# Two adaptive-layernorm layers: moving the clamps, the scaled weights and some statistics to other places of a hand-written order

## The chip, the cores and the metric

One Trainium2 chip; the program runs on one of its cores. The core has TensorE (matrix products; PE in the profile, PEld for its weight loads), VectorE (DVE), ScalarE (ACT), GpSimd (POOL) and SyncE (SP, which here only issues DMAs). The metric is the device time of one execution in microseconds (us); of several runs the median counts.

## The reference

The input x has 8 batches of 512 tokens with 256 features, in float32. Two layers follow each other, each with an attention part and a feed-forward part:

- mod = silu(c) @ wmod gives for each batch six vectors of 256: sa, ca, ga, sb, cb, gb. ga and gb are clamped away from zero: (2 (g >= 0) - 1) * max(|g|, 0.25).
- attention part: h = layernorm(x) * (1 + ca) + sa; x = x + ga * attn(h)
- feed-forward part: h = layernorm(x) * (1 + cb) + sb; x = x + gb * ffn(h)

Layer 0's attention is h + [linear attention, window attention] @ Wout, after an RMS norm of h with the weight norm_w; the linear part has 16 heads of 16 with quadratic features and a causal sum, the window part a softmax over 64 earlier tokens. Since its first term is h itself, layer 0 computes x + ga * h and ga * (...) @ Wout as separate pieces. Its feed-forward part mixes each token with the one before it and computes sigmoid(xr Wr) * (relu(xk Wk)^2 Wv). Layer 1's attention is a causal softmax with rotary positions and a projection. Its feed-forward part is four products through 1024 hidden features.

## The kernel before, in words

The kernel holds one batch at a time in SBUF, 128 tokens or 128 features to a partition. Layer 0 runs through 16 units (a batch and one half of its heads), ten steps each; layer 1 through 32 units of six steps. Three PSUM tiles of two banks (`sc`) take scores and two of one bank (`mm`) take everything else.

The order of all this work is written out by hand. `when(time, what)` (L327) puts a closure on a list, with a time in steps of layer 0; `when1` (L330) does so with steps of layer 1, which begin at layer 0's step 160. At the end the list is sorted by time and carried out under `tc.manual_schedule()` (L1509), so each engine gets its instructions in that order, and each SyncE or GpSimd DMA too. An engine carries out its own instructions strictly in that order; between engines, semaphores make each instruction wait for the data that it needs and for the buffer that it overwrites. The numbers are places in an order and not times.

Batch b of layer 0 begins at step t0 = 20 b. Around it stand:

- `fetch` (L386, x from memory at t0 - 24.5, with the rows sa, ca, ga in `bc` from b = 2 on), `normed` (L349: statistics L357, a reciprocal root by ACT in L339 and L340, its refinement by five small VectorE instructions L344 to L347 and L363, the normalisation L371 on ACT or L373 on VectorE), `modulated` (L420: GpSimd multiplies and adds rows in L429, then forms ga * h in L431 and adds it to x in L433; in batch 0 the first two are VectorE's, L425 and L427), `squares` (L441), the RMS scale `hr` (L453 on VectorE in batch 0, L457 on GpSimd later), the transposes of hr (L468), the projections (L102, copied by `whole` to `qf` in L490) and the value copies `vs` (L543).
- `step` (L667): linear scores (L561), which ACT squares (L572) and GpSimd masks (L576), and window scores (L594), whose row maxima VectorE takes (L605); window weights (L638, ACT L648, GpSimd L658). `lin_values` (L701) and `win_values` (L724) are the products with the values.
- `finish` (L764): `scaled_weights(0)` at t0 + 26.0 fetches ga of the batch, spread over all partitions, into the tile `br` (SyncE, L772) and lets GpSimd form ga * Wout (L775) for the products L798 at t0 + 34.6 to 35.85, which L808 adds to x; `scaled_weights(1)` at t0 + 41.2 does the same with gb and the feed-forward weight. Both use the one `br` tile. `out_of` adds the feed-forward result to x by GpSimd (L908) and writes x to memory (`x_mid`, SyncE, L912, at t0 + 49.4).

The vectors mod are formed in a prologue at steps -22 to 2. The pieces ga and gb of all batches lie as 8x512 rows in `stash`; `clamped_batches(layer)` (L262) clamps them with four VectorE instructions (L220 to L223) and writes them to `mod_dram`, from where `fetch_ga` and `scaled_weights` read. Batch 0's ga is clamped apart, from PSUM, at -12.05. In front of all of that GpSimd sets the ones in four tiles (`vones`, `vswap`: L313, L319) and multiplies the weights Wq, Wk and Wv by norm_w (L317).

Layer 1's `prepare1` (L1047) fetches x by a GpSimd DMA (L1053), and uses `normed` with places of its own (`early` for batches 0 and 1, `usual` for the others); scores are L1214 and L1272, with maxima L1225, the shifted queries `qs` (L1256), ACT's exponentials L1283 and GpSimd's masks L1287; rotations are L1134 and L1139, value products L1306. The first steps of layer 1 run between the last ones of layer 0. After step 192 of layer 1 comes a feed-forward stage that is a long row of TensorE products (L1568).

Of the kernel before, what the change touches and what calls it, by code (L numbers as in the profile page):

```python
# [13 lines left out]
ALU = mybir.AluOpType  # L14
# [4 lines left out]
B, T, D = 8, 512, 256  # L19
H, HD = 16, 16  # L20
NTB = T // P
NC = D // P
# [8 lines left out]
def bcast(ap, shape, axis):  # L31
    return ap.unsqueeze(axis).to_broadcast(list(shape))
# [3 lines left out]
def adaln_two_layers_kernel(ctx: ExitStack, tc: tile.TileContext, t, out):  # L36
    nc = tc.nc
# [3 lines left out]
    def load(pool, name, shape, src, eng=None):  # L41
        dst = pool.tile(list(shape), FP, name=name, tag=name)
        (eng or nc.sync).dma_start(out=dst, in_=src)
        return dst
# [92 lines left out]
    with ExitStack() as lctx:  # L137
# [36 lines left out]
        wq, wk, wv = (wqkv0[:, :, i * D : (i + 1) * D] for i in range(3))  # L174
        normw = load(rp, "normw", [P, NC], t["norm_w_cols"])
# [38 lines left out]
        mod_b = rp.tile([P, NC, T], FP, name="mod", tag="df")[:B, 0, :]  # L214
        clamps = rp.tile([P, NC, T], FP, name="clamps", tag="xk")

        def clamp(dst, src):
            p, n = src.shape
            neg, sgn = clamps[:p, 0, :n], clamps[:p, 1, :n]
            nc.vector.tensor_scalar(neg, src, -1.0, 0.25, ALU.mult, ALU.max)  # L220
            nc.vector.tensor_tensor(neg, neg, src, ALU.max)
            nc.vector.tensor_scalar(sgn, src, 0.0, 2.0, ALU.is_ge, ALU.mult)
            nc.vector.scalar_tensor_tensor(dst, sgn, -1.0, neg, ALU.add, ALU.mult)  # L223

        def mod_product(ps, weights, layer, col, n):

            w, o = wm[layer][col // T], col % T
            for k in range(NC):
                nc.tensor.matmul(ps, weights[:, k, :], w[:, k, o : o + n], start=(k == 0), stop=(k == NC - 1))
# [9 lines left out]
        def by_batches(layer):  # L239
            if layer == 0:  # L240
                ps = got0["rows"] = sc.tile([P, 2, T], FP, name="sc", tag="sc")
                mod_product(ps[:B, 0, :], sT[0], 0, 0, T)
                ps = ps[:B, 1, :]
            else:
                ps = got0["rows"] = mm.tile([P, T], FP, name="mm", tag="mm")
                ps = ps[:B]
            for i, v in enumerate((2, 5)):
                mod_product(ps[:, i * D : (i + 1) * D], sT[layer], layer, v * D, D)

        stash = rp.tile([P, NC, T + 1], FP, name="stash", tag="hf")  # L250
# [8 lines left out]
        def copied_batches(layer):  # L259
            nc.scalar.copy(stash[:B, layer, :T], got0["rows"][:B, 1, :] if layer == 0 else got0["rows"][:B])  # L260

        def clamped_batches(layer):  # L262
            dst = mod_b if layer else mod_a[:, 2:4, :].rearrange("p v d -> p (v d)")
            clamp(dst, stash[:B, layer, :T])
            nc.sync.dma_start(
                out=mod_dram[:, 2 + 2 * layer : 4 + 2 * layer, :], in_=dst.rearrange("p (v d) -> p v d", d=D)
            )
# [42 lines left out]

        vones = [wp.tile([P, NTB, H, 32], FP, name=f"vo{i}", tag=f"vo{i}") for i in range(2)]
        vswap = [rp.tile([P, NTB, H // 2, 32], FP, name=f"vs{i}", tag=f"vs{i}") for i in range(2)]
        nc.gpsimd.memset(vones[0], 1.0)  # L313

        for w in (wq, wk, wv):
            for k in range(NC):
                nc.gpsimd.tensor_scalar(w[:, k, :], w[:, k, :], normw[:, k : k + 1], None, ALU.mult)  # L317
        for v in (vswap[0], vones[1], vswap[1]):
            nc.gpsimd.memset(v, 1.0)  # L319

# [4 lines left out]
        def when(time, what):  # L327
            plan.append((min(time, END0) + STEP0 * max(time - END0, 0.0), len(plan), what))
# [20 lines left out]
        def normed(when, x, first, at_root, last, name, by_act=True):  # L349

            held = {}

            def stats(j):
                if j == 0:
                    held["st"] = tok.tile([P, NTB, 6], FP, name="st", tag="st", bufs=2)
                    held["mv"] = tok.tile([P, NTB, 2], FP, name="mv", tag="mv", bufs=2)
                nc.vector.bn_stats(held["st"][:, j, :], x()[:, j, :])  # L357
                nc.vector.bn_aggr(held["mv"][:, j, :], held["st"][:, j, :])

            def spread():  # L360
                better(held, held["mv"][:, :, 1], 1e-5)
                off = held["off"] = tok.tile([P, NTB], FP, name="off", tag="off", bufs=2)
                nc.vector.scalar_tensor_tensor(off, held["mv"][:, :, 0], -1.0, held["r"], ALU.mult, ALU.mult)  # L363

            def norm(j):
                if j == 0:
                    held["x"] = tok.tile([P, NTB, D], FP, name=name, tag=name)
                dst, src = held["x"][:, j, :], x()[:, j, :]
                r, off = held["r"][:, j : j + 1], held["off"][:, j : j + 1]
                if by_act:  # L370
                    nc.scalar.activation(dst, src, AF.Identity, bias=off, scale=r)  # L371
                else:
                    nc.vector.tensor_scalar(dst, src, r, off, ALU.mult, ALU.add)  # L373

            for j in range(NTB):
                when(first[j], lambda j=j: stats(j))
                when(last[j], lambda j=j: norm(j))
            when(at_root, lambda: root(held, held["mv"][:, :, 1], eps5))
            when(at_root + 0.25, spread)
            return held  # L380

        def prepare(b):
            t0 = 20 * b
# [20 lines left out]
            when(t0 - 24.5, fetch)  # L404
            if b == 1:
                when(t0 - 31.9, fetch_rows)
                when(t0 - 15.9, fetch_ga)
            ln = normed(
                when,
                lambda: xs0[b],  # L410
# [353 lines left out]
        def finish(b):  # L764

            t0 = 20 * b
# [3 lines left out]
            def scaled_weights(i):  # L770
                bc = rp.tile([P, 1, D], FP, name="br", tag="br")
                nc.sync.dma_start(out=bc, in_=mod_dram[b, 2 + i : 3 + i, :].partition_broadcast(P))  # L772
                w, n = ((wout, 4), (wfv, 2))[i]
                held["w", i] = rp.tile([P, n, D], FP, name=f"ws{i}", tag=("xr", "ws1")[i])
                nc.gpsimd.tensor_tensor(held["w", i], w, bcast(bc[:, 0, :], [P, n, D], 1), ALU.mult)  # L775

            when(t0 + 26.0, lambda: scaled_weights(0))
            when(t0 + 41.2, lambda: scaled_weights(1))

            def features(c):  # L780
# [143 lines left out]
        for m in range(2 * B):  # L924
            t0 = 10 * m
# [12 lines left out]
            when(t0 + 20.45, lambda m=m: win_values(m))  # L938

        when(-22.0, on_every_row)  # L940
        when(-21.9, lambda: by_batches(0))
        for i, at in enumerate((-21.85, -13.65, -12.1)):
            when(at, lambda i=i: folded(i))
        for i, at in enumerate((-21.8, -21.7, -12.5, -12.4, -10.3, -6.4)):
            when(at, lambda i=i: mod_features(i))
        when(-12.05, lambda: clamp(ga_all, got0["f"][:, 1, :D]))
        when(-12.0, kept_batches)
        when(-10.4, lambda: copied_batches(0))
        when(1.6, lambda: by_batches(1))
        when(2.05, lambda: copied_batches(1))  # L950
        when(4.05, lambda: clamped_batches(0))
        when(4.95, lambda: clamped_batches(1))
        for b in range(B):
            prepare(b)
            finish(b)
# [91 lines left out]
        def prepare1(b):  # L1047

            t0 = 24 * b
# [3 lines left out]
                nc.gpsimd.dma_start(out=xs1[b], in_=x_mid[b].rearrange("(j p) d -> p j d", p=P))  # L1053


            early = ((135.5, (138.7, 0.3), 139.75, (142.15, 0.4)), (153.0, (164.2, 0.3), 165.6, (166.2, 0.2)))
            usual = (t0 - 37.0, (t0 - 33.6, 1.0), t0 - 29.4, (t0 - 28.6, 0.6))
            if b == 2:
                usual = (*usual[:3], (t0 - 28.9, 0.25))
            if b == 3:  # L1060
                usual = (t0 - 35.6, (t0 - 32.4, 0.6), *usual[2:])
            begin, (first, more), at_root, (last, apart_) = (early + (usual,))[min(b, 2)]
# [131 lines left out]
            for j, at in ((0, t0 + 6.45), (2, t0 + 9.45)):  # L1194
                if b == 0:
                    at = (6.7, 8.7)[j // 2]
# [219 lines left out]
        for b in range(B):  # L1416
            prepare1(b)
            project_out(b)
            for m in range(3 * b, min(3 * b + 3, len(raws))):
                at = 50 + 6 * m  # L1420
                when1(at, lambda m=m: look(m))
                for i in range(2):
                    when1(at + 5.6 + i, lambda m=m, i=i: low_bits(m, i))
# [10 lines left out]
        t0 = 24 * B  # L1434
# [286 lines left out]
```

## Time and profile before

| what | value |
| --- | --- |
| median of three runs | 1816.61 us (1813.01 to 1821.35) |
| profiled execution, its own time | 1810.34 us |
| its span, first to last instruction | 1808.6 us |
| mean granted TensorE clock | 0.993 |
| TensorE busy | 1742.7 us, 96% |
| VectorE, ScalarE, GpSimd busy | 1079.5, 887.3, 722.1 us |
| prologue and first steps, 0 to 90 us | TensorE busy 72.2 us |
| the rest of layer 0, 90 to 630 us | TensorE busy 523.6 us |
| both layers' steps together, 630 to 720 us | TensorE busy 79.5 us |
| layer 1's attention, 720 to 1200 us | TensorE busy 466.4 us |
| feed-forward stage, 1200 to 1808 us | TensorE busy 601.1 us |

A row of a timeline gives the start and the length in us, the engine, the line, the operation, the tiles written and read, the shapes and how many instructions are merged; in brackets stands the idle time in front of the row and who ended it. A row of the table by windows gives the window, its length, the busy time of TensorE, its weight loads, VectorE, ScalarE and GpSimd (instructions in brackets), then the granted TensorE clock as a share of the full one, the share of the DMA engines and GB/s.

### The profile page before, as it was taken

The numbers are of one execution on the slowest core, as the hardware profiler recorded it, in microseconds if no ns is written. First come the engines' busy times: TensorE is split into PE (matmuls) and PEld (weight loads), VectorE is DVE, ScalarE is ACT, GpSimd is POOL, SyncE is SP. The second block draws the span as 40 slices with busy tenths as digits, with TensorE's granted clock in tenths as the row PEclk, the third lists the DMA queues.
The fourth block names the chain that finished last, engine by engine and source line by source line (L and its number), as shares of the span: only waits on it lengthen the run. The fifth ranks groups of instructions, "written<-read, shape, count | busy, mean of one in ns | idle before, by whom it ended". The sixth has DMA issues, their size and how long they took to land.

```text
span 1808.6 us, 41155 instructions
## 1 busy us (share of the span) xinstructions
PE 1742.7 (96%) x16886; PEld 1191.8 (66%) x16886; DVE 1079.5 (60%) x3708; ACT 887.3 (49%) x1276; POOL 722.1 (40%) x1098
## 2 busy tenths in 40 slices
PE   7899999999999988999999999999999999999998
PEld 4456666665666654544555455688888888888887
DVE  5556574756656566578888887435354553635352
ACT  3666666766667645566666665413122222313221
POOL 4675866768576663456655555500000000000000
PEclk9999999999999999999999999999999999999999
DMA  4100101011001101023121110520000000000000
GB/s 149 41 14 6 37 5 37 5 38 33 12 17 35 40 5 39 1 66 117 51 74 52 61 48 30 190 59 27 1 27 26 1 27 1 27 1 27 0 13 14
DMA packets 43029, 65.59 MB, mean 36 GB/s; under 512 B 4152, under 2 KB 33592, under 8 KB 42832
## 3 DMA queue, kind: packets, MB, share of 16 engines
q1 hardware_dynamic: 37648, 46.62, 8.0%
q0 software_dynamic: 5184, 16.25, 3.0%
q8 instruction: 134, 2.20, 0.5%
q14 instruction: 63, 0.52, 0.1%
HBM read 50.24 MB, written 12.63 MB: 35 GB/s over the span
## 4 chain that ended last, share of the span: by engine, by line
PE 56%; ACT 3%; POOL 3%; DVE 2%; issue 1%; DMA 0%; ACTq 0%; POOLq 0%; DVEq 0%
PE mm L1568 31%; PE sc L1272 7%; PE mm L1306 4%; PE mm L1631 3%; PE mm L1124 2%; PE mm L1364 2%; PE mm L1182 2%; PE sc L1214 1%; ACT at L1283 1%; POOL flat L1139 1%; PE sc L1474 1%; POOL at L1287 1%; PE mm L1248 1%; PE mm L798 1%; ACT k L1146 1%
## 5 line engine op out<-in xcount | busy, mean ns | idle before, releaser
L1568 PE MATMUL mm<-gh,h 128*128 128x512 f32 x1024 | 398.1, 390 | 1.8 <-issue 1.8
L1568 PE MATMUL mm<-gl,h 128*128 128x512 f32 x1024 | 397.5, 389 | 0.0
L1225 DVE CUSTOM_DVE_ANT_0 junk<-sc,cmask 128x256 bf16<-128x256 f32 (+3 forms) x512 | 225.2, 487 | 93.5 <-PE sc L1214 90.0
L131 DVE CAST gh<-row 128x512 fp32r<-128x512 f32 x192 | 82.1, 431 | 257.9 <-ACT row L1614 132.3
L1283 ACT ACTIVATE at<-sc 128x768 f32<-128x768 f32 (+1 forms) x192 | 168.8, 882 | 113.9 <-PE sc L1214 101.3
L1568 PEld LDWEIGHTS mm<-gh,h 128*128 128x128 f32 x1024 | 192.2, 188 | 41.9 <-issue 2.2
L1568 PEld LDWEIGHTS mm<-gl,h 128*128 128x128 f32 x1024 | 192.2, 188 | 39.7
L658 POOL TENSOR_SCALAR_AFFINE_SELECT aw<-aw 64x512 f32<-64x512 f32 (+1 forms) x320 | 168.5, 553 | 97.5 <-ACT aw L648 93.8
L572 ACT ACTIVATE at<-sc 128x768 f32<-128x768 f32 (+1 forms) x192 | 164.0, 883 | 65.8 <-PE sc L561 65.1
L1214 PE MATMUL sc<-k,q 32*128 32x512 f32 (+3 forms) x1024 | 190.6, 469 | 5.8 <-ACT at L1283 4.5
L1272 PE MATMUL sc<-qs,k 32*128 32x384 f32 (+3 forms) x1024 | 188.6, 468 | 1.7 <-DVE qs L1256 1.7
L1287 POOL TENSOR_SCALAR_AFFINE_SELECT at<-at 128x256 f32<-128x256 f32 x256 | 103.5, 417 | 186.4 <-ACT at L1283 186.0
L605 DVE CUSTOM_DVE_ANT_0 junk<-sc,wmask 128x128 bf16<-128x128 f32 x512 | 115.3, 285 | 82.6 <-PE sc L594 82.5
L576 POOL TENSOR_SCALAR_AFFINE_SELECT at<-at 128x256 f32<-128x256 f32 x256 | 104.7, 430 | 110.6 <-ACT at L572 109.8
L1620 ACT ACTIVATE row<-mm,h_s_cols 128x512 f32<-128x512 f32 x64 | 44.1, 689 | 194.3 <-PE mm L1568 194.3
L132 DVE TENSOR_TENSOR gl<-row,gh 128x512 fp32r<-128x512 f32 x185 | 127.0, 689 | 7.3
L1272 PEld LDWEIGHTS sc<-qs,k 32*128 32x128 f32 x1024 | 81.3, 184 | 68.4 <-DVE maxima L1225 35.2
L1614 ACT ACTIVATE row<-mm,h_s_cols 128x512 f32<-128x512 f32 x64 | 44.2, 690 | 155.8 <-PE mm L1568 155.7
L561 PE MATMUL sc<-qm,qk 32*128 32x512 f32 (+3 forms) x1024 | 100.3, 470 | 2.4 <-ACT qq L503 1.0
L1214 PEld LDWEIGHTS sc<-k,q 32*128 32x128 f32 x1024 | 82.1, 184 | 14.1 <-ACT at L1283 9.7
L1608 ACT ACTIVATE sg<-mm,w_s_cols 128x512 f32<-128x512 f32 x56 | 38.6, 689 | 103.6 <-PE mm L1568 95.8
L648 ACT ACTIVATE aw<-sc 128x1024 f32<-128x1024 f32 (+1 forms) x64 | 62.2, 972 | 43.7 <-PE sc L638 42.3
(249 smaller groups left out, 3532.8 us busy)
## 6 DMA issues: line engine op xcount, KB each, us to landing
x_mid<-x SPq DMA_DIRECT2D x16, 512.0 KB, 3.0
x<-x_mid POOLq DMA_DIRECT2D x9, 512.0 KB, 4.3
raw<-in_h1T_dram SPq DMA_DIRECT2D x8, 512.0 KB, 3.4
raw<-in_h2T_dram SPq DMA_DIRECT2D x8, 512.0 KB, 3.4
h<-in_h1T_dram POOLq DMA_DIRECT2D x8, 512.0 KB, 7.2
h<-in_h2T_dram POOLq DMA_DIRECT2D x8, 512.0 KB, 7.7
out_dram<-tmp SPq DMA_DIRECT2D x16, 256.0 KB, 2.8
x<-in_L_attn_x_dram SPq DMA_DIRECT2D x7, 512.0 KB, 4.5
```

The source lines that it names most:

```text
L132: (rest or nc.vector).tensor_tensor(parts[1], src, parts[0].bitcast(FP), ALU.subtract)
L561: lambda i=i, r=r, kb=kb, n=n, o=o: nc.tensor.matmul(ps[:, i, o : o + n], k[r, e, kb * P : (kb + 1) * P], qm[r, e, kb * P : T], start=True ...
L572: nc.scalar.activation(at, ps[:, :, :o], AF.Square, scale=0.5)
L576: nc.gpsimd.affine_select(out=d, in_=d, pattern=[[0, 2], [1, P]], compare_op=ALU.is_ge, fill=0.0, base=0, channel_multiplier=-1,)
L605: nc.vector.tensor_tensor_reduce(junk, ps[:, i, ii * P : (ii + 1) * P], wmask[:, int(blk > 0), :], -1.0, BIG, ALU.add, ALU.min, maxima[:, ...
L658: nc.gpsimd.affine_select(out=d, in_=d, pattern=[[0, d.shape[1]], [sign, 64]], compare_op=ALU.is_ge, fill=0.0, base=0, channel_multiplier= ...
L1214: nc.tensor.matmul(ps[:, i, o : o + m], q[r, e, qb * P : (qb + 1) * P], k[r, e, :m], start=True, stop=True,)
L1225: nc.vector.tensor_tensor_reduce(junk[:, :m], ps[:, i, o : o + m], got1["cmask"][:, T - m :], -1.0, BIG, ALU.add, ALU.min, maxima[:, NTB * ...
L1272: nc.tensor.matmul(ps[:, i, o : o + m], k[r, e, kb * P : (kb + 1) * P], qs[r, kb * P : T], start=True, stop=True)
L1283: nc.scalar.activation(at, ps[:, :, :o], AF.Exp, scale=0.25)
L1287: nc.gpsimd.affine_select(out=d, in_=d, pattern=[[0, 2], [1, P]], compare_op=ALU.is_ge, fill=0.0, base=0, channel_multiplier=-1,)
L1568: nc.tensor.matmul(ps, w[:, k, col : col + P], part[:, k, :], start=(k == 0 and i == 0), stop=(k == n - 1 and i == len(parts) - 1),)
```

## The change

It moves work to other places of the order; what is computed stays the same, and no instruction is added or taken away.

- The four memsets of ones stand together; the scalings of Wq and Wk come into the list at -20.2 and that of Wv at -11.1, behind the sums of batch 0.
- Layer 0's clamp goes from 4.05 to -2.7, layer 1's from 4.95 to four places between 5.45 and 7.1, one instruction each, behind the copy qf (5.35).
- Batch 1's ga is read at -2.6 instead of 4.1.
- ga * Wout, with its DMA, goes from t0 + 26.0 to t0 + 30.3 for all batches but the last. That is behind hr, L431 and L433 of batch b + 2 (t0 + 27.4 to 28.8), behind the second L908 and the x_mid write of batch b - 1 (t0 + 29.4); for batch 6 also behind two loads of layer 1 (146.2, 150.0).
- In layer 1 the statistics, roots and, for batch 2, the fetch and the normalisations get other places.

```diff
-        def clamp(dst, src):
+        def clamp(dst, src, steps=range(4)):
...
+            for i in steps:
...
-        def clamped_batches(layer):
+        def clamped_batches(layer, *steps):
             dst = mod_b if layer else mod_a[:, 2:4, :].rearrange("p v d -> p (v d)")
-            clamp(dst, stash[:B, layer, :T])
+            clamp(dst, stash[:B, layer, :T], steps)
+            if 3 not in steps:
+                return
...
-        nc.gpsimd.memset(vones[0], 1.0)
-
-        for w in (wq, wk, wv):
-            for k in range(NC):
-                nc.gpsimd.tensor_scalar(w[:, k, :], w[:, k, :], normw[:, k : k + 1], None, ALU.mult)
-        for v in (vswap[0], vones[1], vswap[1]):
+        for v in vones + vswap:
             nc.gpsimd.memset(v, 1.0)
+
+        def scaled(*ws):
+            for w in ws:
+                for k in range(NC):
+                    nc.gpsimd.tensor_scalar(w[:, k, :], w[:, k, :], normw[:, k : k + 1], None, ALU.mult)
...
-                when(t0 - 15.9, fetch_ga)
+                when(t0 - 22.6, fetch_ga)
...
-            when(t0 + 26.0, lambda: scaled_weights(0))
+            when(t0 + (30.3 if b < B - 1 else 26.0), lambda: scaled_weights(0))
...
+        when(-20.2, lambda: scaled(wq, wk))
+        when(-11.1, lambda: scaled(wv))
...
-        when(4.05, lambda: clamped_batches(0))
-        when(4.95, lambda: clamped_batches(1))
+        when(-2.7, lambda: clamped_batches(0, 0, 1, 2, 3))
+        for i, at in enumerate((5.45, 6.1, 6.7, 7.1)):
+            when(at, lambda i=i: clamped_batches(1, i))
...
-            early = ((135.5, (138.7, 0.3), 139.75, (142.15, 0.4)), (153.0, (164.2, 0.3), 165.6, (166.2, 0.2)))
+            early = ((135.5, (138.7, 0.3), 139.75, (142.15, 0.4)), (153.0, (163.3, 0.3), 164.65, (166.2, 0.2)))
             usual = (t0 - 37.0, (t0 - 33.6, 1.0), t0 - 29.4, (t0 - 28.6, 0.6))
             if b == 2:
-                usual = (*usual[:3], (t0 - 28.9, 0.25))
+                usual = (t0 - 37.8, (t0 - 34.9, 0.45), t0 - 32.2, (t0 - 28.8, 0.45))
```

The four numbers of `early` and `usual` are the place of the fetch, the place and distance of the four statistics, the place of the root, and the place and distance of the four normalisations.

More of the change, by code (lines that the diff above doesn't have):

```diff
@@ L215, in adaln_two_layers_kernel @@
         clamps = rp.tile([P, NC, T], FP, name="clamps", tag="xk")
-        def clamp(dst, src):
+        def clamp(dst, src, steps=range(4)):
             p, n = src.shape
             neg, sgn = clamps[:p, 0, :n], clamps[:p, 1, :n]
[L220 to L223, printed above, removed]
+            for i in steps:
+                if i == 0:
+                    nc.vector.tensor_scalar(neg, src, -1.0, 0.25, ALU.mult, ALU.max)
+                elif i == 1:
+                    nc.vector.tensor_tensor(neg, neg, src, ALU.max)
+                elif i == 2:
+                    nc.vector.tensor_scalar(sgn, src, 0.0, 2.0, ALU.is_ge, ALU.mult)
+                else:
+                    nc.vector.scalar_tensor_tensor(dst, sgn, -1.0, neg, ALU.add, ALU.mult)
         def mod_product(ps, weights, layer, col, n):
```

## The prediction

> **What bounds the kernel now.** I read the share of busy time first, then the busy table by windows with the granted clock, then the list of idle gaps in front of TensorE's instructions, and last the timelines of VectorE, GpSimd and SyncE around the largest gaps.
>
> ```profile
> PE 1742.7 (96%) x16886; PEld 1191.8 (66%) x16886; DVE 1079.5 (60%) x3708; ACT 887.3 (49%) x1276; POOL 722.1 (40%) x1098
> 50.25:55.30 5.05, 0.01 (x2) 0.03 (x2) 4.90 (x11) 0.11 (x1) 2.71 (x6) 0.64 0.10 29
> 55.30:59.30 4.00, 4.00 (x36) 1.49 (x40) 3.49 (x28) 2.43 (x5) 0.00 (x0) 0.60 0.42 135
> 126.80:130.20 3.40, 3.40 (x26) 2.37 (x25) 0.00 (x0) 1.53 (x3) 3.40 (x5) 0.50 0.03 10
> 713.40:717.30 3.90, 3.90 (x20) 1.06 (x24) 1.51 (x7) 3.90 (x8) 1.64 (x2) 0.56 0.02 4
> ```
>
> TensorE is busy for 96% of 1808.6 us. So only its idle 66 us, and the time in which it is busy at half clock (column after POOL's), can be won by moving work of other engines. Four stretches show both at once: a gap, then a granted clock near 0.5 although TensorE is full. The same product of 32 matmuls, L701, takes 3.94 us at 55.30 and 2.36 us at 70.24 (clock 1.00). The change touches the work around each of these gaps.
>
> ```profile
> 45.17 2.57 DVE L222 TENSOR_SCALAR clamps<-stash 8x512 f32<-8x512 f32 x1
> 47.77 2.73 DVE L223 SCALAR_TENSOR_TENSOR mod<-clamps 8x512 f32<-8x512 f32 x1
> 50.53 1.62 DVE L543 COPY vs<-vo 64x256 f32<-64x256 f32 x4
> 54.48 0.67 DVE L490 COPY qf<-mm 128x512 f32<-128x512 f32 x1
> 55.30 1.08 PE L701 MATMUL mm<-at,vo 128*32 128x512 f32 x4 [5.04 <-DVE qf L490]
> 17.52 3.97 DVE L453 TENSOR_SCALAR hr<-h,rr 128x256 f32<-128x256 f32 x4
> 119.23 2.38 POOL L775 TENSOR_TENSOR ws<-L_attn_Wout,br 128x1024 f32<-128x1024 f32 x1
> 119.40 2.22 DVE L344 SCALAR_TENSOR_TENSOR rt<-ss,rr 128x4 f32<-128x4 f32 x1
> 126.51 0.88 PE L468 MATMUL mm<-ident,hr 128*128 128x128 f32 x4 [1.61 <-POOL hr L457]
> 660.39 2.29 DVE L347 TENSOR_TENSOR rr<-rr,rt 128x4 f32<-128x4 f32 x1
> 665.08 1.13 PE L1214 MATMUL sc<-k,q 32*128 32x512 f32 x4 [1.16 <-DVE maxima L1225]
> 710.96 0.91 PE L1272 MATMUL sc<-qs,k 32*128 32x384 f32 x4 [1.71 <-DVE qs L1256]
> 713.37 1.17 PE L1214 MATMUL sc<-k,q 32*128 32x384 f32 x4 [1.49 <-ACT at L1283]
> 212.05 0.37 SPq L912 DMA_DIRECT2D x_mid<-x  x1
> 216.97 0.42 SPq L772 DMA_DIRECT2D br<-mod_dram  x1
> ```
>
> The largest gap, 5.04 us, waits for the copy qf. Two rounds of clamping and the copies vs stand before it in VectorE's order. One clamp step takes 2.57 us beside a GpSimd tensor_tensor and 0.41 us (at 53.43) without one. The 128x4 step of a norm does the same: 2.22 us beside L775, 0.15 to 0.17 us elsewhere. So a VectorE instruction on two SBUF operands, or a plain SBUF to SBUF one, stands until GpSimd's tensor_tensor ends. Those with an operand in PSUM do not: L625 takes 0.69 us inside and outside such a stretch.
>
> **The change, part by part.** The sum is made against the profiled execution (1810.34 us, span 1808.6) and carried over to the median of the runs, 1816.61.
>
> *Prologue.* Three memsets (0.94, 1.80, 0.94 us) move ahead of the weight scalings, into GpSimd's 4.73 us of waiting for Wq: nothing is late for it there. hr (L453, 3.97 us of which 2.6 is standing still behind the last scalings and memsets; alone about 1.4 as L373 shows) is then ready before TensorE has ended the small products in front of it, and the 1.10 us gap at 20.76 goes. wv's scaling (1.82) goes behind the sums of batch 0, ends near 28 and is read at 33.69: hidden by 5 us. The other side: the memsets now run until about 10.1, where L373 (9.63, four of 0.35 us, plain SBUF) would stand; its last piece would start at 11.2, just as the four scalings start (11.21). If it is caught behind them, until 15.2, hr ends 1.7 later than now. Bounds: 1.7 lost, 2.5 won (if the half clock from 20.99 on catches less of L102); I take the gap, 1.1.
>
> *The clamps.* Layer 0's (0.41, 0.7, 0.41, 0.7: 2.3 us) goes to -2.7, behind L499, where VectorE idles 2.62 us before L605 at 36.89, less 1.2 for two statistics: hidden but for some tenths. Its DMA and the read of ga (now at -2.6) stand in SyncE's order ahead of the fetch of batch 2 only, which has 20 us. Layer 1's four steps come behind qf, spread. VectorE then runs L543 straight after the maxima: two of its four copies still stand behind the two L429 (5.0 us in all), as they do in each later batch (2.13 and 2.35 us at 184 and 186), so qf ends near 0.5 us after TensorE is free: 4.5 of 5.04 won. L701 runs at full clock: 1.6. The spread steps can meet hr's and ga's tensor_tensor (1.9 and 2.4) just before the sums are normalised, whose PSUM tile the transposes of hr need: I take 0.6 off, 2.5 at worst. Together 5.5 (2.0 to 6.6).
>
> *ga times Wout later.* Of seven, one matters now: batch 0's at 119.23 blocks L344 (2.07 us lost) and delays hr of batch 2; TensorE idles 0.97 at 123.70 and 1.61 at 126.51. Without it, GpSimd still does six selects (2.60, ready when ACT's exponential ends at 120.0), one of 0.41 and hr (1.89): hr ends near 125.0 instead of 126.45. 1.5 won, and some of the half clock from 126.80 to 130.22 (at most 1.7): 0.5, so 2.0 (0.5 to 4). In batches 1 to 5 GpSimd waits for ACT before hr anyway (1.24 us at 198.87), and TensorE's 0.49 there waits for ACT: nothing won.
> What is moved is also a DMA. br is now issued behind x_mid's (212.05, which waits for the second L908), where it used to be prefetched. GpSimd is free at 212.75; br was on its way 2.84 us alone (174.09 to 176.93) and 4.85 behind a fetch (216.97 to 221.82), so GpSimd stands 3 to 4 us with the next selects behind it, multiplies until about 219.5 and has caught up by 229. The first reader, L798 on ws and cat, comes at 223.53; the sums that need the next selects at 233.04. Batch 6, behind the two rope loads: br lands near 606, product done 608.5, read at 613.02. Hidden by 4 us everywhere; if not, it is the second rival.
>
> *Layer 1, batch 1.* The root a step earlier puts L344 to L363 into a stretch where GpSimd is idle (8.25 us before 659.06) instead of beside L1139 and L775: 4.2 us off VectorE. The 1.16 gap goes, ACT's backlog (3.46 idle for off) too, and with it most of the 1.13 at 670.19: 2.2 (0.5 to 2.8).
>
> *Layer 1, batch 2.* Statistics come 1.3 to 3 steps earlier, so two of them (0.64 each) and a chain of five (0.87) leave VectorE's queue at 702 to 713: qs 0.8 earlier. ACT no longer stands 2.19 us for off before L1283: the 1.49 goes. L1306 took 3.74 at half clock, 2.36 otherwise: 1.4. Together 3.7 (0.8 to 5.5). The earlier fetch waits on x_mid of batch 6, which is written by 680.5; GpSimd gets there near 681.
>
> Sum: 1.1 + 5.5 + 2.0 + 2.2 + 3.7 = 14.5. Profiled: 1795.8. Median: 1816.6 - 14.5 = 1802.1.
>
> **A rule to weigh.** In this trace half clock followed 1.61 us of gap (126.80) and 1.71 + 1.49 us (713.9), and lasted 3.41 or 6.83 us. The Trainium skill, "TensorE: Matmul & The Clock Gate", section "HAM oscillation — how this bites in real kernels", says that idle gaps over about 3.4 us are what throttles the clock. By that rule only the 5.04 us gap would cost clock, and my 0.5 and 1.4 would not come back. The trace speaks against it, in both places.
>
> **Rivals.**
> 1. *The stalls change their owner.* L373 is caught in the prologue (-1.7), the spread clamps collide with GpSimd (2.0 instead of 5.5), batch 2's queue only shifts (0.8 of 3.7). For it: VectorE is 60% busy and every collision costs 2 us. Against it: later batches with the same order, without clamps, show no such gap. -1.7 + 2.0 + 2.0 + 2.2 + 0.8 = 5.3, plus some luck of clock: about 1810.
> 2. *Slower: br comes too late.* L775 must start by 221.0 to be in time for 223.53; br may take 8.5 us from 212.5. If the write and the read of 512 KB around it hold it for 12.5, TensorE stands 4 us in each of six batches, and each gap brings a half clock window (1.7): +34 - 14.5, about 1836. It decides at 8.5 us; the longest seen is 4.85.
> 3. *The clock does not come back for short gaps* (the rule above): 14.5 - 0.5 - 1.4 = 12.6, that is 1804.0.
>
> **How the numbers follow.** Forecast 0.70, rival 1 0.16, rival 2 0.07, rival 3 0.07. A measurement here can tell 0.5%, 9 us, from no change: faster means under 1807.5, slower over 1825.7. The runs of before spread from 1813.0 to 1821.4, and how the clock's windows fall is part of that, so 4 us of chance are added to the terms' own ends: the forecast's bounds are 1791 and 1809. With rival 1 the range is 1791 to 1812. Faster: 0.60 of the forecast, the 0.07 of rival 3 and 0.05 of rival 1, 0.72. Same: 0.20. Slower: 0.08.
>
> **What would show it.** Right: no gap over 1 us at L701 (near 49 us) and full clock after it; L453 at 1.4 us; L344 of batch 2 at 0.16 us and hr's gap under 1.2; L346 to L363 of layer 1's batch 1 at 0.2 us each; no pair of gaps at L1272 and L1214 near 695 to 700; and GpSimd idle 3 to 4 us before six of the L775, with no gap of TensorE at L798. Wrong: a TensorE gap at L798 for ws; h (L373) taking 4 us more; or TensorE's idle time over 60 us.

## The result and the profile after

| | before | after |
| --- | --- | --- |
| median of 15 runs, us | 1817.35 (1810.82 to 1821.47) | 1810.89 (1806.92 to 1819.47) |
| profiled execution, us (span) | 1810.34 (1808.6) | 1810.60 (1808.9) |
| TensorE busy, us | 1742.7 | 1749.4 |
| VectorE, ScalarE, GpSimd busy, us | 1079.5, 887.3, 722.1 | 1066.9, 886.3, 718.4 |

The ratio is 0.9965, 95% interval 0.9952 to 0.9978: 6.4 us faster (4.0 to 8.7), under the 0.5% that counts as a difference in the prediction. The forecast was 14.5. The number lies near the sum of the prediction's first rival (5.3), but not for that rival's reasons, as the last part shows. The profiled execution of before happened to be the fastest of its 15 runs, so the two profiled times alone would show nothing; places and gaps are compared below, and times by medians.

The table by windows of after, at the places shown for before and at two new ones:

```profile
55.90:58.40 2.50, 0.01 (x2) 0.02 (x1) 2.40 (x8) 0.77 (x2) 2.50 (x3) 1.00 0.03 6
59.30:69.60 10.30, 9.82 (x116) 5.86 (x112) 3.29 (x21) 5.44 (x7) 5.51 (x9) 0.50 0.53 154
126.80:130.20 3.40, 3.40 (x152) 2.48 (x153) 0.98 (x2) 2.25 (x3) 3.25 (x7) 1.00 0.29 116
629.40:646.40 17.00, 16.70 (x233) 10.35 (x233) 5.52 (x25) 5.17 (x7) 11.24 (x17) 0.50 0.03 10
713.40:717.30 3.90, 3.73 (x40) 1.53 (x40) 3.03 (x15) 3.75 (x7) 1.70 (x3) 1.00 0.01 4
```

Two of the old half-clock stretches are gone (126.80 and 713.40 now stand at 1.00). Two others took their place: 10.3 us behind a new gap of 2.50 us, and 17 us from 629.40, where before had none. Rows of after's timeline for the steps that went as forecast, wholly or in part:

```profile
17.51 1.14 DVE L462 TENSOR_SCALAR hr<-h,rr 128x256 f32<-128x256 f32 x4
...
123.61 0.55 PE L477 MATMUL mm<-ident,hr 128*128 128x128 f32 x3 [1.19 <-POOL hr L466]
...
661.91 0.16 DVE L353 SCALAR_TENSOR_TENSOR rt<-mv,rr 128x4 f32<-128x4 f32 x1
...
713.57 0.91 PE L1284 MATMUL sc<-qs,k 32*128 32x384 f32 x4 [0.66 <-DVE qs L1268]
```

(Lines are some 9 further down in layer 0, 12 in layer 1.) hr takes 1.14 us instead of 3.97; batch 2's hr waits 1.19 instead of 0.97 + 1.61; layer 1's root steps run at 0.16 us; 0.66 us stands where 1.71 and 1.49 stood. And the rows of what was not forecast:

```profile
46.27 0.83 DVE L222 TENSOR_SCALAR clamps<-stash 8x512 f32<-8x512 f32 x1
54.67 1.96 DVE L226 TENSOR_SCALAR clamps<-stash 8x512 f32<-8x512 f32 x1
56.66 0.77 DVE L228 SCALAR_TENSOR_TENSOR mod<-clamps 8x512 f32<-8x512 f32 x1
58.41 0.63 PE L477 MATMUL mm<-ident,hr 128*128 128x128 f32 x4 [2.50 <-DVE rows L766]
...
602.95 2.40 POOL L784 TENSOR_TENSOR ws<-L_attn_Wout,br 128x1024 f32<-128x1024 f32 x1 [6.03 <-DMA br<-mod_dram]
605.31 0.76 POOL L585 TENSOR_SCALAR_AFFINE_SELECT at<-at 128x256 f32<-128x256 f32 x2
...
627.43 0.33 PE L837 MATMUL mm<-ident,hr 128*128 128x128 f32 x1 [0.37 <-DVE hr L382]
628.70 0.33 PE L837 MATMUL mm<-ident,hr 128*128 128x128 f32 x1 [0.94 <-DVE hr L382]
629.36 1.33 PE L837 MATMUL mm<-ident,hr 128*128 128x128 f32 x5 [0.33 <-DVE hr L382]
...
767.53 0.37 SPq L921 DMA_DIRECT2D x_mid<-x  x1
772.55 0.79 POOL L1065 DMA_DIRECT2D x<-x_mid  x1 [2.73 <-DMA x_mid<-x]
773.83 1.06 PE L1318 MATMUL mm<-at,vo 128*32 128x512 f32 x8 [1.98 <-POOL at L1299]
```

In before the same places read:

```profile
601.02 0.41 POOL L576 TENSOR_SCALAR_AFFINE_SELECT at<-at 128x256 f32<-128x256 f32 x1 [0.51 <-ACT at L572]
...
631.02 1.09 PE L828 MATMUL mm<-ident,hr 128*128 128x128 f32 x6 [1.06 <-DVE hr L373]
...
773.88 2.36 PE L1306 MATMUL mm<-at,vo 128*32 128x512 f32 x32 [0.52 <-POOL at L1287]
```

The 5.04 us gap is gone, but two of the spread clamp steps (1.96 and 0.77 us) now stand in front of the rows for which TensorE waits 2.50 us. ga times Wout of batch 6 stands 6.03 us on GpSimd for br. Near 627 there are three gaps, 1.64 us in sum, where before had one of 1.06. And near 772 a load of layer 1 waits 2.73 us on GpSimd's queue for the write of x_mid, with the masks behind it: 1.98 us instead of 0.52.

By the times at which the same matmul starts, after leads by 4.92 us at the hr of batch 1 (63.33 against 58.41). Behind the 10.3 us of half clock 1.4 of it is left, at 93 us. After leads by 4.07 at the hr of batch 3, by 2.3 at 628.70, and stands 5.26 behind at the end of the 17 us of half clock; layer 1's two batches bring that back to a lead of 1.5 at 730, and the gap near 772 takes it.

### The profile page after: what moved, and what is told of

Same layout as the page of the kernel before. It is cut to its first block, busy times and chain, and to the rows that moved or that the text cites. A ratio compares the mean times of both kernels' runs of the same rounds, so it can differ in the third digit from the quotient of the medians.

```text
span 1808.9 us, 41154 instructions
## 1 busy us (share of the span) xinstructions
PE 1749.4 (97%) x16886; PEld 1196.1 (66%) x16886; DVE 1066.9 (59%) x3708; ACT 886.3 (49%) x1276; POOL 718.4 (40%) x1098
## 4 chain that ended last, share of the span: by engine, by line
PE 82%; ACT 7%; POOL 4%; DVE 3%; issue 2%; DMA 1%; SPq 0%; ACTq 0%; POOLq 0%
PE mm L1580 31%; PE sc L1284 7%; PE mm L807 5%; PE mm L102 4%; PE mm L710 4%; PE mm L1318 4%; PE sc L570 4%; PE mm L1643 3%; PE mm L1136 2%; PE sc L647 2%; PE mm L1376 2%; PE mm L1194 2%; PE mm L733 2%; PE mm L535 2%; PE sc L1226 1%
## 5 line engine op out<-in xcount | busy, mean ns | idle before, releaser
L1226 PEld LDWEIGHTS sc<-k,q 32*128 32x128 f32 x1024 | 82.2, 184 | 11.7 <-ACT at L1295 8.3
```

What stands on the lines that cost most here:

```text
L1226: nc.tensor.matmul(ps[:, i, o : o + m], q[r, e, qb * P : (qb + 1) * P], k[r, e, :m], start=True, stop=True,)
```

## The experiments

Each run lists its span and its mean granted clock. Span x clock is roughly the time at full clock; span x (1 - clock) is the lost clock. The second is right where TensorE is busy through the half clock; a gap inside it moves a part from one to the other. The means over a kernel's runs:

| kernel | median us (runs) | ratio to before, 95% | span x clock | lost clock |
| --- | --- | --- | --- | --- |
| before, beside the others | 1816.21 (85) | | 1794.8 | 20.1 |
| after | 1810.89 (15) | 0.9965, 0.9952 to 0.9978 | 1790.4 | 19.7 |
| before_again | 1817.72 (12) | 1.0009, 0.9994 to 1.0023 | 1794.0 | 21.9 |
| prologue_only | 1819.85 (12) | 1.0005, 0.9992 to 1.0018 | 1795.1 | 21.7 |
| clamps_only | 1813.41 (12) | 0.9988, 0.9974 to 1.0001 | 1792.7 | 18.6 |
| ga_only | 1819.50 (12) | 1.0023, 1.0003 to 1.0043 | 1796.5 | 22.8 |
| layer1_only | 1808.89 (12) | 0.9957, 0.9940 to 0.9974 | 1791.5 | 15.5 |
| layer1_batch2 | 1809.69 (12) | 0.9974, 0.9960 to 0.9988 | 1792.9 | 16.3 |
| late_signs | 1803.96 (8) | 0.9945, 0.9926 to 0.9964 | 1789.0 | 14.0 |
| ga_first | 1804.15 (6) | 0.9932, 0.9908 to 0.9955 | 1788.6 | 14.1 |
| ga_but_last | 1807.86 (8) | 0.9951, 0.9932 to 0.9969 | 1789.8 | 14.7 |
| ga_never | 1807.12 (6) | 0.9954, 0.9935 to 0.9972 | 1788.2 | 17.2 |
| ga_split | 1808.39 (7) | 0.9959, 0.9944 to 0.9974 | 1790.4 | 16.8 |
| late_and_first | 1801.43 (6) | 0.9922, 0.9901 to 0.9943 | 1788.1 | 12.3 |
| later_and_first | 1799.86 (6) | 0.9908, 0.9893 to 0.9924 | 1786.6 | 11.4 |
| later_split | 1802.32 (5) | 0.9912, 0.9893 to 0.9931 | 1789.9 | 10.4 |
| later_never | 1802.04 (5) | 0.9915, 0.9897 to 0.9932 | 1787.7 | 13.3 |
| later_old_prologue | 1799.14 (4) | 0.9898, 0.9877 to 0.9918 | 1786.8 | 11.7 |

The clock is listed to 0.001, 1.8 us in one run; the means of span x clock have standard errors of 0.2 to 0.7, those of lost clock of 0.6 to 2.4 (the largest ga_only's and later_old_prologue's).

### The kernel before once more

No edit.

> The kernel before, unchanged, to learn the granted clock of its runs. The product span x mean clock is roughly the time that a run would take at full clock (profiled execution of before: 1808.6 x 0.993 = 1796.0; after: 1808.9 x 0.990 = 1790.8, 5.2 less). Theory 1 (the change won TensorE's idle time and no clock): the product is 1796 in all runs within 1.5, the mean clock is 0.989 to 0.990 like after's 0.9893, and the spread of the times is the clock's. Theory 2 (the forecast's clock terms of 3.5 us came back): the mean clock is 0.987 to 0.988, 0.002 lower than after's.

Span x clock is 1794.0, the other runs of before give 1794.8, and after 1790.4. Over the 85 runs of before, times go from 1809.84 to 1823.46 and clocks from 0.994 to 0.985, with a correlation of -0.91 (after's 15: -0.98). So nearly all of the spread is clock. The mean clock of these 12 runs, 0.9879, lies where theory 2 put it, but that of all 85 runs of before is 0.9889, and after's is 0.9891: lost clock 20.1 and 19.7. By the larger number after won about 4 us of TensorE's idle time and next to no clock, theory 1. What the later kernels show is that this zero is a sum of gains and losses of over 3 us each.

### The parts alone

prologue_only is before with the memsets and scalings in their new places, clamps_only the two clamps and the read of batch 1's ga, ga_only and layer1_only as follows:

```diff
-            when(t0 + 26.0, lambda: scaled_weights(0))
+            when(t0 + (30.3 if b < B - 1 else 26.0), lambda: scaled_weights(0))
```
```diff
-  (153.0, (164.2, 0.3), 165.6, (166.2, 0.2))
+  (153.0, (163.3, 0.3), 164.65, (166.2, 0.2))
...
-                usual = (*usual[:3], (t0 - 28.9, 0.25))
+                usual = (t0 - 37.8, (t0 - 34.9, 0.45), t0 - 32.2, (t0 - 28.8, 0.45))
```

> Of the change only the memsets ahead of the weight scalings and Wv's scaling behind the sums of batch 0. Theory 1: hr of batch 0 takes under 1.6 us instead of 3.97, the 1.10 us gap before its transposes goes and 0.4 comes before the small products; span x clock 0.5 to 1 lower than before's 1794.3. Theory 2 (the plain pieces of batch 0's normalisation are caught behind the scalings): 1.7 higher.

hr takes 1.14 us, as theory 1 has it, and nothing is caught behind the scalings. But no gain in time can be seen: 0.9 us slower (3.3 slower to 1.5 faster), span x clock 0.3 above that of the other runs of before. hr's gap of about 1.1 us is there in five of the eight profiles with the old order (0.66 to 1.13) and absent in three, where one of the root's steps rather than hr stood behind the memsets (in before_again L346 took 2.64 us). With the new order a 0.38 us gap comes before the small products in some. The clock takes part here too: in after the products L102 start at 22.58 instead of 24.59, but run at half clock and take 6.67 us instead of 5.28, so that at 30 us 0.6 of the lead of 2.0 is left.

> Of the change only the move of the two clamps and of batch 1's read of ga. Theory 1 (the spread steps collide): the 5.04 us gap at the first value product is under 0.8, a new gap of 2 to 2.7 us stands before the transposes of batch 1's hr, ended by the normalised rows; span x clock is 2.5 to 3.2 below before's, time 2 to 4 us below. Theory 2 (the forecast: 4.5 of gap less 0.6, and 1.6 of clock): no gap over 1 us at those transposes, span x clock 3.9 lower, time 5.5 lower.

```profile
59.56 0.66 PE L475 MATMUL mm<-ident,hr 128*128 128x128 f32 x2 [2.50 <-DVE rows L764]
```

Theory 1: the new gap comes with the clamps alone, 2.50 us, and span x clock falls by 2.1, somewhat less than its 2.5 to 3.2 and far less than the forecast's 3.9.

> Of the change only ga times Wout 4.3 steps later, in batches 0 to 6. Theory 1 (it wins at batch 0 and gives it back late): before batch 2's hr transposes 1.2 us of gap instead of 0.97 + 1.61; GpSimd stands 3.8 to 6 us for br in batches 1 to 6; before the transposes of the last feed-forward hr near 630 the gaps add to 1.6 instead of 1.06; the write of x_mid near 768 takes over 4 us and the gap behind it is 1.5 to 2. Span x clock 1793.5 to 1795, against 1794.3 of before: no gain. Theory 2 (the forecast: cover of 4 us everywhere): 1.5 lower, 1792.8, with 0.5 of clock on top.

```profile
778.17 1.88 PE L1306 MATMUL mm<-at,vo 128*32 128x512 f32 x6 [2.23 <-POOL at L1287]
```

Theory 1: batch 2's gap is 1.19, and the three gaps near 630 (0.48, 0.95, 0.33) and this one of 2.23 give it back. The part alone is slower, by 4.2 us (0.5 to 7.8); span x clock is 1.7 above before's, more than theory 1 had.

> Of the change only the places of layer 1's batches 1 and 2. Theory 1 (the 1.98 us gap near 772 in after, behind a GpSimd load that waits for the write of x_mid, belongs to the luck of that write, 4.50 us against 3.03): the 1.16, 1.13, 1.71 and 1.49 us gaps fall to under 1.5 in sum, the gap near 772 is 0.5, span x clock is 3.5 to 4.5 lower than before's and the time 3.5 to 5 lower. Theory 2 (a write takes its time whatever runs ahead of it, and the earlier arrival only waits there): the gap near 772 is 1.5 to 2.5 again and the time is 2 to 3 lower.

Theory 1 for the gap near 772, which is 0.51 here; the four gaps of 5.5 us in sum are replaced by two of 0.66 and 0.68. But the time falls by 7.8 us (4.7 to 10.9), more than either theory, since the lost clock falls from 20.1 to 15.5.

### Layer 1's batch 2 alone

Only the second of the two edits above.

> Of the change only layer 1's batch 2. Theory 1 (the pair of gaps 1.71 and 1.49 calls a half-clock stretch in most runs, and both parts go together): gaps of 0.66 and under 0.4 in their place, the 1.16 and 1.13 of batch 1 stay; span x clock 2 to 2.6 lower, lost clock 3 to 5 less, time 5 to 7 lower than before. Theory 2 (the forecast: 2.3 of gap and 1.4 of clock): 3.7 lower.

The table by windows of before_again (first fence) and of this kernel, 40 us around the pair of gaps:

```profile
705.00:745.00 40.00, 35.63 (x250) 17.65 (x249) 26.79 (x104) 21.94 (x35) 15.72 (x24) 0.87 0.00 1
```
```profile
700.00:740.00 40.00, 37.66 (x295) 20.17 (x293) 27.34 (x104) 23.98 (x37) 18.59 (x27) 1.00 0.00 1
```

The granted clock goes from 0.87 to 1.00 and some 45 more matmul instructions fit into the stretch. Span x clock falls by 1.9, lost clock by about 3.8; the ratio says 4.7 us (2.2 to 7.3). That lies between the two theories, and the forecast's 3.7 is inside the interval; the two means lie nearer theory 1 than the forecast's split of 2.3 gap and 1.4 clock.

### The clamp steps moved on

late_signs is after with this edit; later_and_first has 12.0 and 12.05 in the place of 9.7 and 9.75, and ga times Wout later in batch 0 alone (see below):

```diff
-        for i, at in enumerate((5.45, 6.1, 6.7, 7.1)):
+        for i, at in enumerate((5.45, 6.1, 9.7, 9.75)):
```

> After, with the last two clamp steps of layer 1 at 9.7 and 9.75 instead of 6.7 and 7.1, behind the first normalisation and the shifted queries. Theory 1 (those two steps make the 2.50 us gap: 1.96 and 0.77 us on VectorE in front of the rows): the gap before batch 1's hr transposes falls under 0.6, span x clock is 1.9 to 2.5 lower than after's 1790.8, time 8 to 9.5 below before's. Theory 2 (the rows wait for something else, such as the transposes of the sums or GpSimd's own queue): a gap over 1.5 stays and the time is after's, 6.5 below before's.

```profile
58.81 1.65 DVE L226 TENSOR_SCALAR clamps<-stash 8x512 f32<-8x512 f32 x1
60.99 2.23 DVE L228 SCALAR_TENSOR_TENSOR mod<-clamps 8x512 f32<-8x512 f32 x1
```

The gap before hr falls from 2.50 to 0.50: those two steps made it. They still meet GpSimd, now the forming of batch 1's h and x (57.82 to 62.68), and hold the second qs (at 63.15), for which TensorE waits 1.24 us. So span x clock falls by 1.4 only; the rest of the 7 us is clock.

> After with ga times Wout later in batch 0 alone and the last two clamp steps of layer 1 at 12.0 and 12.05, where GpSimd has no tensor_tensor (at 9.7 they stood 1.65 and 2.23 us behind the forming of batch 1's h and x, and held the shifted queries for a gap of 1.25). If VectorE's standing behind GpSimd is the whole cost of those steps: 0.4 and 0.7 us each, no gap over 0.8 between 53 and 70 us, span x clock 0.8 to 1.3 lower than with 9.7, 1786.8 to 1787.3; time 1798 to 1802. Rival (the new place delays the sums of batch 0's second half): a gap of 1 to 2 us near 72 and no gain.

With the steps at 12.0 and 12.05, where GpSimd does selects, they take:

```profile
67.44 0.57 DVE L226 TENSOR_SCALAR clamps<-stash 8x512 f32<-8x512 f32 x1
68.05 1.01 DVE L228 SCALAR_TENSOR_TENSOR mod<-clamps 8x512 f32<-8x512 f32 x1
```

No gap between 53 and 70 is over 0.73, and span x clock is 1.5 under that of late_and_first. It is the fastest version together with later_old_prologue: 16.7 us below before (13.8 to 19.4), below after by about 11.

### Where ga times Wout costs

ga_first, ga_but_last and ga_never are after with `b == 0`, `b < B - 2` and never as the condition for 30.3:

```diff
-            when(t0 + (30.3 if b < B - 1 else 26.0), lambda: scaled_weights(0))
+            when(t0 + (30.3 if b == 0 else 26.0), lambda: scaled_weights(0))
```

> After, with ga times Wout later in batch 0 alone and at its old place in batches 1 to 6. Theory 1 (only batch 0 gains; batch 6's, which stands 6.03 us on GpSimd, puts 1.5 to 2 us of backlog into the rotations near 618 and so 0.6 us of gap near 627; and the slow write near 768 comes with it): the last feed-forward hr has one gap of 1.06, the write takes 3.0 us with 0.5 of gap behind it; span x clock 1.5 to 2.3 under after's 1790.4. Theory 2 (those two gaps belong to the other parts, or to luck): the gaps of 1.6 and near 2.0 stay, span x clock within 0.5 of after's.

```profile
626.29 1.09 PE L837 MATMUL mm<-ident,hr 128*128 128x128 f32 x6 [1.06 <-DVE hr L382]
```

Theory 1, in both places: one gap of 1.06 here, and 0.52 before the value products. Span x clock is 1.8 lower than after's and lost clock 5.6 lower.

> After with both mends: the last two clamp steps of layer 1 at 9.7 and 9.75, and ga times Wout later in batch 0 alone. If both theories hold, span x clock is 1789.0 (that of the first mend alone) less 1.5 to 2.3, so 1786.7 to 1787.5, and at a mean clock of 0.990 to 0.992 the time is 1803 to 1807, 10 to 13 below before's. If the second mend does nothing it is the first alone: 1789.

Both mends together are 0.9922, but span x clock is 1788.1, above the expected 1786.7 to 1787.5: the 1.25 us gap of qs is still there, which the next mend (later_and_first) took away.

> After, with ga times Wout later in batches 0 to 5 and at its old place in batch 6 too. Theory 1 (batch 6's is the one that costs, because layer 1's first rotations and selects stand behind it on GpSimd): one gap of 1.06 us before the last feed-forward hr, none of 1.6 to 2.2 near 765, span x clock 1788 to 1789.2 and 5 to 6 us less of lost clock than in after, like the kernel with batch 0 alone; time 1803 to 1806. Theory 2 (the 3.8 to 5.3 us that GpSimd stands in each of batches 1 to 5 cost as much): span x clock near after's 1790.4 and time 1808 to 1811.

Between the theories. Batch 6 makes the three gaps (one of 1.05 here), but the write near 759 still takes 3.72 us and the gap behind it is 1.21. That part belongs to batches 1 to 5.

> After, with ga times Wout at its old place in all batches. Theory 1 (batch 0 alone wins, 1.4 us of gap): the gaps of 0.97 and 1.61 are back before batch 2's hr transposes, span x clock 1.2 to 1.6 above the kernel with batch 0 alone, so 1789.8 to 1790.4, some clock lost behind the 1.61; time 1806 to 1808, still under after's 1810.9. Theory 2 (batch 0's move wins nothing either): time and span x clock as with batch 0 alone, 1804 and 1788.6.

The 0.97 and 1.61 us gaps are back and the median is 3.0 over ga_first's, as theory 1 has it, with intervals that overlap; span x clock does not show it (1788.2), lost clock does (17.2 against 14.1). Its median is 3.8 under after's, again with intervals that overlap. That the part as a whole loses is what ga_only shows.

The slow write near 768 can be followed in the trace. All DMA packets of the first 3 us of it, in after and, second fence, in before:

```profile
q1 hardware_dynamic: 502, 0.50, 49.7%
q8 instruction: 1, 0.02, 3.3%
```
```profile
q1 hardware_dynamic: 527, 0.52, 57.1%
```

In after a packet of 16 KB of instructions starts 0.75 us behind the write's issue and takes 1.59 us. By 3 us 502 of the write's 527 packets have started; the last ones follow one by one until 4.08, and the write lands after 4.50 us instead of 3.03. In before the packet starts 2.69 us behind the issue, at the write's end. Over all kernels: where ga times Wout is later in batches 1 to 5 (eight profiles) the packet starts 0.64 to 1.27 us in and the write takes 3.72 to 4.76; in the other twelve it starts at 2.7 to 3.05 and the write takes 3.03 to 3.06. In all 20 the write is slow where the packet comes early, and only there. In those eight, TensorE's own queue has 117 or 118 semaphore instructions up to there instead of 111 or 112: six products wait for ws that used to be done long before. That these move the place at which the next piece of code is fetched is argued, not shown. The Trainium skill, "Runtime: NRT & Kernel Launch", section "Instruction fetch mechanics", says that code comes in blocks of 16 KiB, 256 instructions, by an engine's own DMA queue, and that crossing a block is mostly hidden. The block's size agrees with the packet's 16384 bytes; here it was not hidden, for another queue's write.

### The DMA or the product

ga_split is after with the read of ga back at 26.0 in all batches and only the product at 30.3; later_split has the clamp steps at 12.0 as well.

```diff
+            when(t0 + 26.0, lambda: fetched_row(0))
             when(t0 + (30.3 if b < B - 1 else 26.0), lambda: scaled_weights(0))
```

> After, with the read of ga into br back at t0 + 26.0 in all batches and only the product ga times Wout at t0 + 30.3. Theory 1 (the cost of batches 1 to 6 is the moved DMA: GpSimd stands 3.9 to 6.0 us for br): GpSimd stands under 0.5 us there, one gap of 1.06 before the last feed-forward hr near 627, span x clock 1788.2 to 1789.4, time 1803 to 1807. Theory 2 (the product itself is in the wrong place in batches 1 to 6): the gaps of 1.65 and near 2 stay and the time is 1808 to 1811.

```profile
598.96 2.42 POOL L789 TENSOR_TENSOR ws<-L_attn_Wout,br 128x1024 f32<-128x1024 f32 x1
...
766.15 0.79 POOL L1071 DMA_DIRECT2D x<-x_mid  x1 [2.26 <-DMA x_mid<-x]
```

GpSimd no longer stands for br, and the three gaps are one of 1.06: those come from the moved DMA. The slow write stays (4.03 us): it comes with the moved product. Theory 1 is right on the gaps near 627 and wrong on the sum: 1808.4, and span x clock is after's, although the gaps of both places are 1 us shorter; where that went is open.

> The same with the last two clamp steps of layer 1 at 12.0 and 12.05. Theory 1: as the fastest so far (1799.9, span x clock 1786.6), within 2. Theory 2: 4 to 7 us slower than that.

2.5 over later_and_first, between the theories; lost clock is as low (10.4), span x clock 3.3 higher, of which the gap of 1.54 behind the write is the part that the trace shows.

> The fastest so far (clamp steps at 12.0, ga times Wout later in batch 0 alone: 1799.9) with batch 0's at its old place too. Theory 1 (batch 0's move wins 1.4 us of gap and the half clock behind the 1.61): 2 to 4 us slower, 1802 to 1804. Theory 2 (that gap is filled from a later slack): within 1, 1799 to 1801.

2.2 over later_and_first, theory 1's side, but 0.9915 and 0.9908 have overlapping intervals. That batch 0's move is worth its place rests on the gap (1.19 against 0.98 + 1.61) and on the clock below.

> The fastest so far with the memsets and weight scalings of the prologue as before. Theory 1 (the 1.10 us gap before batch 0's hr transposes comes only in some executions, and the 0.4 before the small products takes its place): within 1 of 1799.9. Theory 2 (the forecast's 1.1): 1801 to 1802.

Theory 1: 1799.1 against 1799.9. The prologue's part can be left out.

### Where the clock goes

> After once more, one look, to see where its half clock falls. Theory 1 (the three gaps near 627, 1.65 us in sum, call it): half clock within 625 to 650 again, 3.4 to 17 us of it; 6.8 to 14 us behind the 2.50 us gap between 55 and 75; none between 110 and 200. Theory 2 (the 17 us at 629 were luck): none between 600 and 700. The gaps of 2.50, of 1.65 in three and near 2.0 before the value products near 772 are there in both.

> The kernel with only ga times Wout later, one more look. Theory 1: no half clock between 110 and 200 again (before, which has the 0.97 and 1.61 us gaps there, had 3.4 and 10.2 us), and some between 600 and 700 or behind the gap near 776. Theory 2 (where half clock falls is luck): half clock between 110 and 200 too.

after_again took 1811.68 us, ga_only_again 1816.83. Half clock starts at 629.9 and 632.1, right behind the three gaps, and again at 773.2 and 778.9, behind the gap at the value products; both have none between 110 and 200. Theory 1 in both. Over the 20 profiles, the length of half clock by place (us; the time lost is half of it):

| place | with the gap | without |
| --- | --- | --- |
| 45 to 110 | 5.04 us: mean 8.3 (6.8 to 10.2, 7 profiles); 2.50 us in its place: mean 9.8 (3.4 to 13.7, 7 profiles) | neither: 3.4 in all 6 |
| 110 to 200 | 0.97 + 1.61 us: mean 6.8 (3.4 or 10.2, 8 profiles) | 1.19 us: none in all 12 |
| 600 to 700 | three gaps: mean 8.2 (0 to 17.1, 5 profiles) | one of 1.06: mean 1.8 (0 to 10.2, 15 profiles) |
| 700 to 745 | 1.71 + 1.49 us: mean 8.5 (6.8 or 10.2, 6 profiles) | 0.66 us: mean 2.2 (0 to 6.8, 14 profiles) |

A place with 1.6 to 3.2 us of gaps so costs 3.2 to 3.4 us of clock on top of them, on average. In one execution it need not: of the five profiles with the three gaps, ga_only has no half clock between 600 and 700, and later_old_prologue has 10.2 us there with one gap. One place goes the other way. Near 20 us every profile has half clock, 6.8 us of it in the eleven with a gap of 0.38 to 1.13 us there and 10.2 in the nine with none over 0.3. Why is open; it means that the absence of a gap in the prologue is no gain by itself.

The Trainium skill, "TensorE: Matmul & The Clock Gate", section "HAM oscillation — how this bites in real kernels", puts the limit at idle gaps over about 3.4 us. All gaps of this table but the 5.04 are shorter; by that limit their columns would be alike, and they are not.

## Why the prediction was wrong

The steps, in us won; measured is the part alone, from its ratio.

| step | forecast | measured (95%) |
| --- | --- | --- |
| prologue | 1.1 | -0.9 (-3.3 to 1.5) |
| clamps | 5.5 | 2.2 (-0.2 to 4.7) |
| ga times Wout | 2.0 | -4.2 (-7.8 to -0.5) |
| layer 1, both batches | 5.9 | 7.8 (4.7 to 10.9) |
| sum | 14.5 | 4.9; all together 6.4 (4.0 to 8.7) |

Of the 9.6 us between the two sums, 6.2 is ga times Wout, 3.3 the clamps and 2.0 the prologue; layer 1 won 1.9 more than its forecast.

*ga times Wout* is the step that failed, in its sign. The price of br was somewhat low (GpSimd stood 3.9 to 6.0 us; the prediction said 3 to 4), but the first reader L798 was not late, and the second rival did not happen. What failed is "Hidden by 4 us everywhere". It asked only who reads ws and when the next selects are needed. In batch 6, behind which layer 1's first rotations stand on GpSimd, the select that started at 601.02 in before starts at 605.66 (the second of two in the row at 605.31), although TensorE was 2.8 us ahead; VectorE gets to the last feed-forward root only 0.95 earlier (624.87, 623.92), and TensorE, which kept its lead until then, waits three times. With the read of br alone back at its old place (ga_split) one gap of 1.06 stands there again, so it is the wait for br that makes the three. The write behind the packet of code was not thought of at all. And the clock of batch 2, taken as 0.5, is 3.4 (6.8 us of half clock to none). By the traces the step would be worth about 4.8 in batch 0 alone (an estimate: 1.4 of gap and 3.4 of clock); the medians with and without it differ by 2.2 and 3.0, with intervals that overlap. In batches 1 to 6 it loses more than that: after's median is 6.7 over ga_first's.

*The clamps.* The 4.5 us of the big gap came. "I take 0.6 off, 2.5 at worst" was mis-sized: the worst came true, a gap of 2.50. The 1.6 us of L701 at full clock came too, and went again, since the new gap calls as much half clock as the old (9.8 against 8.3 us). The first rival had this step at 2.0; 2.2 was measured. Its reason, the spread steps that meet GpSimd's tensor_tensor, is shown by late_signs and later_and_first. That its whole sum of 5.3 lies near the measured 6.4 is luck: it had ga times Wout at 2.0 won and layer 1 at 3.0, against 4.2 lost and 7.8 won, and its L373 in the prologue was not caught.

*Layer 1* was right in mechanism and short in clock: the traces show 1.6 of gap in batch 1 and 2.5 in batch 2 (against 2.2 and 2.3), and 3.2 of clock instead of 1.4.

*The prologue's* gap of 1.10 us is not there in every execution: it is absent in three of eight profiles, and those have 3.4 us more half clock at that place. In after, hr was ready in time, as forecast, and the half clock then fell on more of L102, where the prediction's upper bound had it fall on less. The loss that it feared, L373 caught behind the scalings, did not come.

*The third rival*, that clock doesn't come back for short gaps, is refuted by the table of half clock, most plainly between 110 and 200: half clock in all 8 profiles with the short gaps, in none of the 12 without. The forecast had the right sign and took too little.

## What to carry to other kernels

When an operation with a DMA in front of it is moved behind others on an in-order engine, ask not only when its first reader comes but what is queued behind its wait, up to the next place where that engine is tight; the last batch before a change of stage is where the backlog shows. A place with 1.6 to 3.2 us of gaps cost some 3.2 us of clock on top here, on average, so judge a gap with its clock, and from several profiles. And when VectorE work whose operands all lie in SBUF is spread out, place each piece where GpSimd has no tensor_tensor: the same two instructions took 2.73 and 3.88 us in two wrong places and 1.58 in a right one.

## What the runs showed of the hardware

- Half clock comes in multiples of 3.41 us (all stretches but the one at the very end of each profile), and a stretch of it may be 3.4 us or 17 behind the same gaps (17.1 in after, 3.4 and 6.8 further on in after_again). The smallest gaps with half clock behind them in every profile are those of 0.5 to 1.25 us between 45 and 110 (3.4 us in all six); the 1.19 us near 120 had none behind it in 12 profiles.
- A plain VectorE instruction of 8x512 on SBUF takes 0.41 us alone (53.43 in before), 0.57 beside GpSimd's selects (later_and_first) and up to 2.57 beside its tensor_tensor (2.57 in before, 1.96 in after, 1.65 in late_signs).
- In the eight profiles with a 16 KB packet of instructions early inside a 512 KB write, the whole write was 0.7 to 1.7 us later than in the other twelve, and with it the load that waits for it and the queue of the engine that issues the load.
